# A GNN kernel on one core: one edge tile in 75 of the two relation passes fetched by 128 row DMAs on ScalarE's queue

## The chip, the core and the metric

One core of one Trainium2 chip runs one program. Its engines are TensorE (PE; PEld is its weight load), VectorE (DVE), ScalarE (ACT), GpSimd (POOL) and SyncE (SP), and 16 DMA engines move data between the chip's memory and the core. Each engine works through its own queue of instructions in program order and waits on semaphores. The metric is the device time of one execution in microseconds (us); lower is better.

## What is computed

A graph with N = 30,000 nodes of 128 features and E = 960,000 edges, sorted by destination. Two layers, both with a layer norm, a relu and a residual:

```python
h = relu(layernorm(x))
# layer 0, run twice (basis1, then basis2 on relu of the first result): the two relation passes
W   = einsum('rb,bdf->rdf', coeff, basis)          # 32 relations from 8 bases
msg = einsum('nd,rdf->nrf', h, W)[src, etype] * norm
agg = segment_sum(msg, dst, N) + bias
# layer 1: the gate pass, 4 edge types
msg = sigmoid(k[dst] + q[src]) * v[src];  out = mean over types of (segment_sum(msg, dst) + x @ Ws + b)
```

The part that matters here: for every edge of a relation pass, the feature row of its source node has to be fetched from a table in memory.

## The kernel before

After a short preparation (up to 190 us) three passes over all edges follow: c1 (relation pass 1, reads table h0), c2 (relation pass 2, reads h1) and g (the gate). Only c1 and c2 are changed.

**Tiles.** 128 edges make a tile (TP), 3 tiles a group (G), 5 groups a block (S), 5 blocks a stage (SB; 25 groups, 75 tiles = NTS), 4 stages a loop iteration (NQ), and each pass is a loop of 25 iterations (NI). So a pass has 7,500 tiles, 2,500 groups, 500 blocks and 100 stages. The 384 sorted edges of a group fall into a window of 32 neighbouring destination nodes. The order of work within an iteration is written out by hand: the body below is unrolled, and each engine gets its instructions in that order.

**A group, in `rel_body`.** GpSimd issues three gathers (L118): each takes a column of 128 source indices and fetches 128 rows of 512 bytes into one third of the tile hg, which has 5 buffers, that is 15 gathers. VectorE builds for each tile a matrix sb (L476, 12 buffers): edge by (basis, window column), filled with the edge's coefficient. TensorE multiplies hg by sb and adds the group's three tiles in the PSUM tile pa (L481, 3 buffers). ScalarE copies pa into the block's tile ab (L485). A gather can start when the matmuls of the group five earlier have released its hg buffer; a matmul needs its gather, its sb and a free pa.

**A block.** After the second group of block s+1, TensorE runs the 8 basis matmuls of block s (bases_out, L440), which read the whole ab of block s. VectorE later adds the result into the aggregate (L374). In c1 each block also needs its relation types: four SP DMAs load er for block s+2 at the start of block s (types, L397), VectorE turns er into a one-hot at the fourth group of block s (L405), TensorE multiplies it by the coefficients (L410), and ScalarE stores half of the result for pass 2 (keep, L430). In c2 that result is read back by one SP DMA a block (L435).

**Beside it.** Every 9 or 10 groups a node step of 120 finished nodes is spread over the next groups (`after_first`, `after_second`): transposes, activations on ScalarE (L608, L617; in c2 L653, L661, L672, L685) and stores on ScalarE's queue (L621; in c2 two of L692). SP loads the index tiles of a stage one stage ahead (L351, L357). Eight semaphores are handed in turn to the DMAs of SP and ScalarE: a DMA waits until the eighth before it, in the order in which the program was written, has landed.

The loop over the groups of a block, cut:

```python
for j in range(G):
    gather(hg[:, j, :], table, idx[:, t0 + j:t0 + j + 1])
...
nc.scalar.copy(ab[s][:, :, g, :], pa)
if g == 1 and s:
    bases_out(s - 1)
...
beside(s * S + g)
```

Of the kernel before, what the change touches and what calls it, by code (L numbers as in the profile page):

```python
# [9 lines left out]
F32 = mybir.dt.float32  # L10
I32 = mybir.dt.int32
# [10 lines left out]
N = 30000  # L22
# [8 lines left out]
TP = 128  # L31
NT = E // TP
G = 3
# [3 lines left out]
S = 5  # L37
SB = 5
NQ = 4
NS = NQ * SB  # L40
NGS = S * SB
NTS = NGS * G
# [8 lines left out]
LEAD = 3 * VB  # L51
GAP = 8
EPS = 1e-5
CH = 5
PX, KX = 120, 10
IN_RANGE = "destinations are node numbers, below N"


def rows_of(col, n):
# [13 lines left out]
def kernel(  # L73
# [29 lines left out]
    nc = tc.nc  # L103
# [192 lines left out]
    def sorted_path():  # L296
# [5 lines left out]
        with ExitStack() as all_:  # L302
# [57 lines left out]
            def bases(t, engine):  # L360
# [2 lines left out]
                    min_val=0, max_val=N - 1, skip_runtime_bounds_check_because=IN_RANGE)  # L363
                return vals

            def edge_row(row, i, s, n):

                return bass.AP(tensor=row.tensor, offset=(i * NG + s * S) * GE,
                               ap=[[0, n], [GE, S], [1, GE]])
# [6 lines left out]
            def rel_body(table, weights, second):  # L376
# [4 lines left out]

                def body(bas, i, io, pool, ps, cp, iw, ic, beside):
                    stage = {}
                    er, oh, pc, ce, ce_next, ab, po, base = {}, {}, {}, {}, {}, {}, {}, {}

                    def loads(k):
                        stage[k] = [stage_tile(io, "idx", src, I32, i, k),
                                    stage_tile(io, "relc", reld, F32, i, k),
                                    firsts(io, i, k)]
                        if not second:  # L390
                            stage[k].append(
                                stage_tile(io, "nrm", norm, F32, i, k, 4 * TQ - S * G))

                    def types(s):
                        er[s] = pool.tile([P, TQ, TP], I32, name="er")
                        for c in range(TQ):
                            nc.sync.dma_start(  # L397
                                er[s][:, c, :],
                                bass.AP(tensor=et32_row.tensor,
                                        offset=(i * NG + s * S) * GE + c * TP,  # L400
                                        ap=[[TQ * TP, 4], [0, R], [1, TP]]))

                    def onehot(s):
                        oh[s] = pool.tile([P, TQ, TP], F32, name="oh")
                        nc.vector.tensor_scalar(oh[s], er[s], icol4, None, op0=ALU.is_equal)  # L405
                        at = TQ * 8 * B
                        pc[s] = cp[:TP, at:2 * at].rearrange("p (c q l b) -> p c q l b", c=TQ, q=4,
                                                             l=2)
                        for c in range(TQ):
                            nc.tensor.matmul(pc[s][:, c].rearrange("p q l b -> p (q l b)"),  # L410
                                             lhsT=oh[s][:, c, :],
                                             rhs=coeff.rearrange("p q l b -> p (q l b)"),
                                             start=True, stop=True)

                    def coefficients(s):
                        t0 = s % SB * S * G
                        nrm = stage[s // SB][-1][:, t0:t0 + 4 * TQ]
                        for to, l in ((ce, 0), (ce_next, 1)):
                            to[s] = pool.tile([TP, 4, TQ, B], F32, name=f"ce{l}")
                            nc.vector.tensor_mul(  # L420
                                to[s], pc[s][:, :, :, l].rearrange("p c q b -> p q c b"),
                                nrm.rearrange("p (q c) -> p q c", q=4).unsqueeze(3).to_broadcast(
                                    [TP, 4, TQ, B]))
                            to[s] = to[s].rearrange("p q c b -> p (q c) b")

                    def block_rows(s):
                        return ce2[ds(i * NS + s, 1)].rearrange("o p e -> (o p) e")

                    def keep(s):
                        nc.scalar.dma_start(block_rows(s), ce_next[s][:, :S * G, :].rearrange(  # L430
                            "p t b -> p (t b)"))

                    def kept(s):
                        ce[s] = pool.tile([TP, S * G, B], F32, name="ce", bufs=4)
                        nc.sync.dma_start(ce[s].rearrange("p t b -> p (t b)"), block_rows(s))  # L435

                    def bases_out(s):
                        po[s] = ps.tile([P, S, W], F32, name="po")
                        for b in range(B):
                            nc.tensor.matmul(po[s].rearrange("p s w -> p (s w)"),  # L440
                                             lhsT=bas[:, b, :],
                                             rhs=ab[s][:, b].rearrange("p s w -> p (s w)"),
                                             start=(b == 0), stop=(b == B - 1))

                    loads(0)
                    if second:
                        kept(0)
                        kept(1)
                    else:
                        types(0)  # L450
                        onehot(0)
                        coefficients(0)
                        types(1)
                        onehot(1)
                    for s in range(NS):
                        k = s // SB
                        if s % SB == 0:
                            if s:
                                tc.stage_boundary()
                            if k + 1 < NQ:  # L460
                                loads(k + 1)
                        if s % SB == 2:
                            leave_stage()
                        idx, relc, start = stage[k][:3]
                        if s + 2 < NS:
                            (kept if second else types)(s + 2)
                        ab[s] = pool.tile([P, B, S, W], F32, name="ab")
                        for g in range(S):
                            t0 = (s % SB * S + g) * G
                            hg = pool.tile([TP, G, D], F32, name="hg", bufs=5)  # L470
                            for j in range(G):
                                gather(hg[:, j, :], table, idx[:, t0 + j:t0 + j + 1])
                            pa = ps.tile([P, B, W], F32, name="pa", bufs=3)
                            for j in range(G):
                                sb = pool.tile([TP, B, W], F32, name="sb", bufs=12)
                                nc.vector.scalar_tensor_tensor(  # L476
                                    sb, iw[:TP].unsqueeze(1).to_broadcast([TP, B, W]),
                                    relc[:, t0 + j:t0 + j + 1],
                                    ce[s][:, g * G + j, :].unsqueeze(2).to_broadcast([TP, B, W]),
                                    op0=ALU.is_equal, op1=ALU.mult)  # L480
                                nc.tensor.matmul(pa.rearrange("p b w -> p (b w)"),  # L481
                                                 lhsT=hg[:, j, :],
                                                 rhs=sb.rearrange("p b w -> p (b w)"),
                                                 start=(j == 0), stop=(j == G - 1))
                            nc.scalar.copy(ab[s][:, :, g, :], pa)  # L485
                            if g == 1 and s:
                                bases_out(s - 1)
                            if g == 2 and not second and s + 1 < NS:
                                coefficients(s + 1)
                            if g == 3 and not second:  # L490
                                keep(s)
                                if s + 2 < NS:
                                    onehot(s + 2)
                            if g == 3 and s > 1:
                                add_windows(po[s - 2], base[(s - 2) // SB], s - 2)
                            if g == 3 and s % SB == 1:
                                base[k] = bases(start, DVE)
                            beside(s * S + g)
                    bases_out(NS - 1)
                    for s in (NS - 2, NS - 1):  # L500
                        add_windows(po[s], base[NQ - 1], s)
# [500 lines left out]
```

## Time and profile before

| What | us |
|---|---|
| median of 10 runs (lowest to highest) | 33,972.54 (33,958.92 to 34,021.55) |
| the profiled execution, its own time | 33,968.25 |
| its span, first to last instruction | 33,966.5 |
| c1: first to last gather start | 190.2 to 11,532.2 |
| c2: first to last gather start | 11,566.9 to 22,437.6 |
| gate pass: first to last gather start | 22,483.3 to 33,934.9 |

The profile is of one execution. In its lists of instructions a row gives the line, the engine, the operation, out<-in by tile name and the count; then busy time, the mean of one, and the idle time just before them with what ended it. "issue" means that nothing the profile shows was waited for, "remote" that a semaphore event without a matching instruction ended the wait. POOLq, SPq and ACTq are instructions of the queues themselves, such as issuing a DMA. The ends of matmuls are modelled, so TensorE's times are rough.

### The profile page before, as it was taken

What the parts mean: (1) busy time and instruction counts of PE and PEld (TensorE: products, weight loads), DVE (VectorE), ACT (ScalarE), POOL (GpSimd) and SP (SyncE); (2) the same over time, 40 slices, a digit from 0 to 9 for tenths busy, and PEclk for the clock granted to TensorE, in tenths of its full rate; (3) what the DMA queues carried; (4) which work ended last, traced back from release to release, by engine and by line L of the source; (5) the groups of instructions that cost most, each with busy time, mean ns of one, the idle gap of its engine ahead of it and who ended that gap; (6) DMA issues with size and microseconds to landing.
All of it is one profiled execution on the core that took longest, in us unless ns stands there. A gap on an engine that the chain in (4) does not pass through costs nothing.

```text
span 33966.5 us, 321519 instructions
## 1 busy us (share of the span) xinstructions
PE 19883.3 (59%) x83304; PEld 16939.1 (50%) x83304; DVE 12380.0 (36%) x32695; ACT 3633.4 (11%) x9834; POOL 21302.7 (63%) x22514
## 2 busy tenths in 40 slices
PE   4555555555555566666666666655555555555555
PEld 3444444444444444444444444445555555555555
DVE  3333333333333333333333333333333333333333
ACT  1000000000000011111111111111111111111111
POOL 5666666666666666666666666666666666666665
PEclk8777777777777777877777777765555555555555
DMA  3222222222222222222222222234444444444444
GB/s 98 63 63 64 64 64 64 63 62 65 64 64 64 66 66 66 66 67 66 66 66 66 66 67 66 67 98 125 124 124 124 124 124 125 124 124 124 124 124 120
DMA packets 2171202, 2914.97 MB, mean 86 GB/s; under 512 B 684764, under 2 KB 1617880, under 8 KB 2169544
## 3 DMA queue, kind: packets, MB, share of 16 engines
q0 software_dynamic: 840000, 1967.52, 21.8%
q1 hardware_dynamic: 923347, 651.19, 6.6%
q10 hardware_dynamic: 406197, 276.11, 2.8%
q8 instruction: 802, 13.14, 0.2%
q14 instruction: 856, 7.01, 0.1%
HBM read 2618.79 MB, written 274.16 MB: 85 GB/s over the span
## 4 chain that ended last, share of the span: by engine, by line


## 5 line engine op out<-in xcount | busy, mean ns | idle before, releaser
L118 POOL DMA_INDIRECT hg<-h,idx x15000 | 14186.9, 946 | 8223.8 <-issue 4295.6
L481 PE MATMUL pa<-sb,hg 128*128 128x256 f32 x30000 | 9196.2, 464 | 6068.2 <-issue 3822.4
L481 PEld LDWEIGHTS pa<-sb,hg 128*128 128x128 f32 x30000 | 6891.9, 239 | 7875.0 <-issue 4269.9
L118 POOL DMA_INDIRECT qv<-qvtab,qi x7500 | 7088.8, 945 | 4408.5 <-issue 2284.9
L476 DVE SCALAR_TENSOR_TENSOR sb<-cp,relc,ce 128x256 f32<-128x256 f32 x15000 | 6139.6, 477 | 5429.8 <-remote 4443.3
L549 PE MATMUL po<-sel,msg 128*128 128x32 f32 x15000 | 3456.2, 387 | 4606.2 <-DVE msg L547 3852.9
L549 PEld LDWEIGHTS po<-sel,msg 128*128 128x128 f32 x15000 | 3419.6, 327 | 4896.6 <-DVE msg L547 4020.3
L538 PE MATMUL pk<-kw,oh 128*128 128x128 f32 x15000 | 3969.1, 438 | 142.3 <-issue 97.7
L579 DVE TENSOR_TENSOR pk<-pk,qv 128x384 f32<-128x384 f32 x2500 | 1408.3, 563 | 7093.4 <-remote 5123.6
L485 ACT COPY ab<-pa 128x256 f32<-128x256 f32 x5000 | 1810.4, 373 | 19841.0 <-remote 9586.4
L538 PEld LDWEIGHTS pk<-kw,oh 128*128 128x128 f32 x15000 | 3463.1, 331 | 145.0 <-issue 145.0
L440 PE MATMUL po<-ab,bas 128*128 128x160 f32 x16000 | 2517.5, 313 | 418.4 <-issue 275.9
L440 PEld LDWEIGHTS po<-ab,bas 128*128 128x128 f32 x16000 | 2429.5, 201 | 543.7 <-issue 324.9
L374 DVE TENSOR_TENSOR agg<-agg,po 128x32 f32 x7500 | 1404.0, 187 | 2608.9 <-ACT xs L653 672.0
L580 ACT ACTIVATE pk<-pk 128x384 f32<-128x384 f32 x2500 | 1187.4, 475 | 9392.8 <-DVE pk L579 6157.5
L676 PE MATMUL bank<-wall,hT 128*120 128x512 f32 x1524 | 1042.7, 807 | 944.8 <-DVE kt L687 275.8
L547 DVE TENSOR_TENSOR msg<-pk,qv 128x384 f32<-128x384 f32 x2500 | 1370.2, 549 | 0.0
L410 PE MATMUL cp<-coeff,oh 128*128 128x64 f32 x4000 | 653.7, 304 | 782.7 <-issue 610.3
L525 DVE TENSOR_TENSOR oh<-kb,cp 128x1920 f32<-128x1920 bf16 x500 | 1073.2, 2146 | 47.6 <-issue 31.9
L410 PEld LDWEIGHTS cp<-coeff,oh 128*128 128x128 f32 x4000 | 653.6, 228 | 860.2 <-issue 763.4
L687 DVE TENSOR_TENSOR kt<-bank,ball 120x512 f32<-120x512 f32 x254 | 175.7, 692 | 2267.4 <-PE bank L676 946.7
L676 PEld LDWEIGHTS bank<-wall,hT 128*120 128x120 f32 x1524 | 350.1, 247 | 1278.5 <-issue 629.7
(77 smaller groups left out, 3381.5 us busy)
## 6 DMA issues: line engine op xcount, KB each, us to landing
hg<-h,idx POOLq DMA_INDIRECT x15000
kb<-kcode SPq DMA_DIRECT2D x500, 480.0 KB
kw<-ktab SPq DMA_DIRECT2D x2500, 64.0 KB
er<-in_et_row SPq DMA_DIRECT2D x2000, 64.0 KB
qvtab<-qvt ACTq DMA_DIRECT2D x254, 480.0 KB
qv<-qvtab,qi POOLq DMA_INDIRECT x7500
ktab<-kt ACTq DMA_DIRECT2D x254, 240.0 KB
ce<-ce ACTq DMA_DIRECT2D x500, 60.0 KB
```

The lines of the kernel that those rows point to most:

```text
L118: nc.gpsimd.indirect_dma_start(out=to, out_offset=None, in_=table, in_offset=bass.IndirectOffsetOnAxis(ap=idx, axis=0))
L374: nc.vector.tensor_add(to, to, po[:, g, :])
L410: nc.tensor.matmul(pc[s][:, c].rearrange("p q l b -> p (q l b)"), lhsT=oh[s][:, c, :], rhs=coeff.rearrange("p q l b -> p (q l b)"), start= ...
L440: nc.tensor.matmul(po[s].rearrange("p s w -> p (s w)"), lhsT=bas[:, b, :], rhs=ab[s][:, b].rearrange("p s w -> p (s w)"), start=(b == 0), ...
L476: nc.vector.scalar_tensor_tensor(sb, iw[:TP].unsqueeze(1).to_broadcast([TP, B, W]), relc[:, t0 + j:t0 + j + 1], ce[s][:, g * G + j, :].uns ...
L481: nc.tensor.matmul(pa.rearrange("p b w -> p (b w)"), lhsT=hg[:, j, :], rhs=sb.rearrange("p b w -> p (b w)"), start=(j == 0), stop=(j == G ...
L485: nc.scalar.copy(ab[s][:, :, g, :], pa)
L538: nc.tensor.matmul(pk[n][:, j, :], lhsT=oh[n // S][:, n % S, j * TP:(j + 1) * TP], rhs=kw[n], start=True, stop=True)
L547: nc.vector.tensor_mul(msg, pk[n], qv[n][:, :, 1, :])
L549: nc.tensor.matmul(po[s][:, g, :], lhsT=msg[:, j, :], rhs=sel[s][:, g * G + j, :], start=(j == 0), stop=(j == G - 1))
L579: nc.vector.tensor_add(pk[n], pk[n], qv[n][:, :, 0, :])
L676: nc.tensor.matmul(bank(a, VB, T * D), lhsT=hT, rhs=wall[:, a].rearrange("p t f -> p (t f)"), start=True, stop=True)
```

## The change

In each stage of both relation passes the last of the 75 tiles is no longer gathered by GpSimd. At the stage's first group SP loads that tile's 128 indices into a row (ix). After the copy of each of the first 21 groups (NGX), ScalarE issues 6 or 7 DMAs, one row of 512 bytes each, from the table into a tile hx; before every 16th row it loads 16 indices into registers. The matmul of the last tile reads hx in the place of hg. The other passes and all arithmetic stay.

```diff
+XR = 16
+NGX = NGS - 4
...
+            def last_tile(io, pool, table, array, i, k):
+                ix = io.tile([1, TP], I32, name="ix")
+                nc.sync.dma_start(
+                    ix, array[:, ds(i * (NQ * NTS) + (k + 1) * NTS - 1, 1)].rearrange("p o -> o p"))
+                to = pool.tile([TP, table.shape[1]], F32, name="hx")
+                vals = []
+
+                def fetch(n):
+                    for p in range(n * TP // NGX, min((n + 1) * TP // NGX, TP)):
+                        if p % XR == 0:
+                            _, vals[:] = nc.values_load_multi_w_load_instructions(
+                                ix[:, p:p + XR], engines=[mybir.EngineType.Activation], min_val=0,
+                                max_val=table.shape[0] - 1,
+                                skip_runtime_bounds_check_because=IN_RANGE)
+                        nc.scalar.dma_start(to[p:p + 1, :], table[ds(vals[p % XR], 1), :])
+
+                return to, fetch
...
                             hg = pool.tile([TP, G, D], F32, name="hg", bufs=5)
+                            rows = [hg[:, j, :] for j in range(G)]
+                            if t0 == 0:
+                                last[k] = last_tile(io, pool, table, src, i, k)
+                            if t0 + G == NTS:
+                                rows[-1] = last[k][0]
                             for j in range(G):
-                                gather(hg[:, j, :], table, idx[:, t0 + j:t0 + j + 1])
+                                if t0 + j + 1 < NTS:
+                                    gather(rows[j], table, idx[:, t0 + j:t0 + j + 1])
...
-                                                 lhsT=hg[:, j, :],
+                                                 lhsT=rows[j],
...
                             nc.scalar.copy(ab[s][:, :, g, :], pa)
+                            last[k][1](s % SB * S + g)
                             if g == 1 and s:
                                 bases_out(s - 1)
```

More of the change, by code (lines that the diff above doesn't have):

```diff
@@ L53 @@
 EPS = 1e-5
+XR = 16
+NGX = NGS - 4
 CH = 5
 PX, KX = 120, 10
-IN_RANGE = "destinations are node numbers, below N"
+IN_RANGE = "the edges' ends are node numbers, below N"
 def rows_of(col, n):
@@ L383, in body @@
                     stage = {}
-                    er, oh, pc, ce, ce_next, ab, po, base = {}, {}, {}, {}, {}, {}, {}, {}
+                    er, oh, pc, ce, ce_next, ab, po, base, last = {}, {}, {}, {}, {}, {}, {}, {}, {}
                     def loads(k):
```

## Prediction

> **What bounds the kernel now.** I began with the page's groups by cost and its line of engine totals, to see which engine sets the pace of a pass.
>
> ```profile
> PE 19883.3 (59%) x83304; PEld 16939.1 (50%) x83304; DVE 12380.0 (36%) x32695; ACT 3633.4 (11%) x9834; POOL 21302.7 (63%) x22514
> ...
> L118 POOL DMA_INDIRECT hg<-h,idx x15000 | 14186.9, 946 | 8223.8 <-issue 4295.6 <-remote 2207.4 <-PE pa L481 1206.4
> ```
>
> No engine is full. But GpSimd's gathers of the two relation passes are 14,186.9 us of work with 8,223.8 us of idle time before them: together they fill the 22,212.7 us from the first gather to the last of each pass (190.2 to 11,532.2 and 11,566.9 to 22,437.6). Of the idle time 4,295.6 us is "issue": the fixed pause of some 0.30 us after each gather. Next the timeline of GpSimd's queue around 5,000 us, which shows the rhythm.
>
> ```profile
> 5004.94 0.94 POOL L118 DMA_INDIRECT hg<-h,idx  x1 [0.31 <-issue]
> 5006.19 0.95 POOL L118 DMA_INDIRECT hg<-h,idx  x1 [0.30 <-issue]
> 5010.95 0.94 POOL L118 DMA_INDIRECT hg<-h,idx  x1 [3.82 <-remote]
> 5012.20 0.94 POOL L118 DMA_INDIRECT hg<-h,idx  x1 [0.30 <-issue]
> ```
>
> A gather every 1.25 us, then a stall of 3.8 us, then gathers again. From 5,010.95 to the next stall it is 15 gathers, one block, exactly the five buffers of hg. Over a pass the pitch is 11,342.0/7,499 = 1.512 us in c1 and 10,870.7/7,499 = 1.450 us in c2, so a block takes 22.7 and 21.7 us, of which 15 x 1.25 = 18.75 are gathers and 3.9 and 3.0 stalls. GpSimd waits there for TensorE to release hg. So the bound is a loop: gathers at their own pace as far as the buffers reach, then a wait for the slower side (TensorE, VectorE, ScalarE), once a block.
>
> **The change, removed.** Per stage one gather; 200 in both passes. At the unhindered pitch 200 x 1.25 = 250 us. Ends: 100 x 1.512 + 100 x 1.450 = 296 us if stalls shrink with the gathers, and 0 if the other side of the loop sets the block, since then only the stall grows. I take 250: the trace's gathers stand back to back within a run.
>
> **Added on ScalarE.** No single-row DMA stands on ScalarE's queue before. These are the nearest rows: one-row DMAs on SP (firsts, L357), full tiles on ScalarE (L430), and the one register load on ScalarE (L251).
>
> ```profile
> L357 SPq DMA_DIRECT2D firsts<-in_first_st x300: 3/284/714, 188.0 to 33722.6; - x150
> ...
> L430 ACTq FUSED_REGOPS  x500: 52/55/60, 224.4 to 11535.2; - x167
> ...
> L430 ACTq MOVE ce<-ce x500: 29/29/35, 224.7 to 11535.4; - x167
> L430 ACTq DMA_DIRECT2D ce<-ce x500: 337/338/389, 224.8 to 11535.5; - x167
> ...
> L251 DVEq TENSOR_LOAD <-flag x1: 1908/1908/1908, 174.8 to 174.8; - x1
> L251 ACTq TENSOR_LOAD <-flag x1: 1281/1281/1281, 179.3 to 179.3; - x1
> ```
>
> The columns are least/median/greatest ns. A row needs an address (start to start of the next instruction 84 ns), a move (70 ns), the DMA and about 40 ns to the next: 0.194 + 0.284 = 0.478 us with SP's median; 0.25 us for the DMA (its shorter undisturbed cases) gives 0.444, ScalarE's 0.338 gives 0.532. I take 0.478, since size, not engine, separates the two rows. 128 rows are 61.2 us. Eight register loads of 16 values: 8 x 1.281 = 10.2 us (ends: 8 x 0.478, SP's load of the same flag, = 3.8; 8 x 1.846, VectorE's median for 25 values, = 14.8). So 71.4 us a stage, in 21 of its 25 groups. Those last 21 x 4.54 = 95 us in c1 and 21 x 4.35 = 91 us in c2. The engine's own work there is small (1,014 us busy in 11,300 of c1, 1,160 in 10,800 of c2), and register work and DMA issues run while a copy runs. ScalarE becomes some 75 to 85% occupied in those groups. It does not become the bound by sum, only by order: each copy now stands behind 6 or 7 rows of the group before.
>
> A page speaks here. The Trainium skill, "DMA: Bandwidth & Descriptors", section "Latency and other measured facts", puts the floor of a register load at about 0.6 us; ScalarE's one row here shows 1.281, and the measurement decides. With the page's figure the loads would be 4.8 us a stage in place of 10.2. Its section "Issuing engines are not separate DMA queues" says that starting DMAs from several engines saves only the sequencer's time of starting them, which it calls usually small; here the row of L118 shows 0.946 us of that time for a gather.
>
> **What waits behind the rows.** TensorE needs the copies in two places: pa has three buffers, and the basis matmuls L440 read ab of the whole block. I replayed the trace's start times of ScalarE's instructions with 6 or 7 rows (and the register loads) put behind every copy. A copy starts 2.2 us (c1) and 2.5 us (c2) later on average, at worst some 9 us in 99 of 100. That is later than the trace's matmul three groups on in 8% and 13% of groups, by 0.08 and 0.24 us a group averaged over all; and L440 would start 0.59 us later a block in c1 and 0.67 in c2. As full prices, since L440 stands in front of the matmuls that release the hg buffer that the gathers wait for: 500 x 0.59 + 500 x 0.67 = 630 us. Ends: 0 (the wait that releases hg ends later than L440 anyway) and, with the slow ends of row and load (0.532 and 1.85), 500 x 1.23 + 500 x 1.72 = 1,475 us. I take 630, nearest to the rows chosen.
>
> **SP's queue.** The index row is one more DMA a stage: it is issued after er's at the first group and has from 1 us (the first stage of an iteration) to 28 us and more before the copy that it is needed behind; bounds 0 and 25 x 2 x 5 us = 250, taken as 0. More serious: the eight shared DMA semaphores tie SP to ScalarE. Before, the last er DMA of block s+2 was issued 37.5 us (median, least 19.8) ahead of its one-hot. After, it must wait until the first rows of the group before block s have landed.
>
> ```profile
> 5014.37 0.37 ACT L485 COPY ab<-pa 128x256 f32<-128x256 f32 x1 [2.83 <-PE pa L481]
> ...
> 5017.12 0.48 DVE L405 TENSOR_SCALAR oh<-er,icol 128x512 f32<-128x512 int32 x1
> ```
>
> The copy is that of the last group of block s-1; the one-hot of block s+2 starts 2.8 us after it (median of the trace; 4.6 in the upper quarter). Four er DMAs cannot be issued and landed in 2.8 us: SP's own DMA row L397 has a median of 549 ns and its moves go up to 1.6 us. So this one-hot will wait perhaps 5 to 10 us a block in c1. It costs nothing as long as VectorE's next sb of that block waits for TensorE anyway, as in the block shown, where it starts 16 us later. Bounds 0 and 450 x 10 = 4,500 us; in the forecast 0, in the third case below more.
>
> **Sum.** -250 + 630 = +380 us on the execution's 33,968 us: 34,350 us. That execution is 4 us under the median of the runs, so the sum holds for the median too.
>
> **Rivals.** (1) The rows hide altogether: TensorE's release of hg does not depend on the copies at the margin. For it: within a run GpSimd never waits for ScalarE (36 us of waits on L485 in c1), the stalls cluster at 2 to 3.5 us whatever precedes them, and ScalarE's register and DMA instructions show no slow cases (52/55/60). Then -250 us, 33,720 us. (2) Gain and delay cancel: half of L440's delay counts, -250 + 315 = +65, 34,030 us. (3) The one-hot's wait comes on the path: VectorE stands at L405, and sb, L410 and the adds behind it. It decides from the point where er lands later than VectorE would have gone on, about 16 us after L405. At 3 us for each of 450 blocks: +1,350 on top, some 35,700 us. Against it: the slack shown. (4) The change does not do what it says: the instruction order shows 74 gathers a stage in place of 75 and 512 row DMAs an iteration on ScalarE, so I give this nothing.
>
> **Chances.** Forecast 0.44; (1) 0.33; (2) 0.10; (3) 0.13. About 0.2% (68 us) is what a measurement can tell from no change. Faster is case (1), 0.33; same is case (2), 0.10; slower is the forecast and (3), 0.57. The forecast's own range is 34,050 to 35,200 (380 less 300 from half the delay hidden, and 1,475 - 250 at the slow ends). The range over the cases reaches down to case (1), 33,690, and up to 35,200, leaving out case (3) and a few hundredths on either side.
>
> **What would show it.** Right: GpSimd's gathers 14,800 with the same 0.945 us, stalls a block longer than 3.9 and 3.0 us; TensorE's L440 and L481 idle before them with ScalarE as releaser, more than the 1,200 us of now; a row DMA of 0.28 to 0.34 us and a register load near 1.3 us on ScalarE. Wrong, for case (1): the pitch of the gathers within a run unchanged and the stalls no longer, the passes 125 us shorter each. For case (3): waits of VectorE's L405 on the DMA er, now 19 us in all, in the thousands, in c1 alone. A row DMA that costs 0.1 us, or one that ScalarE has to wait for, would make the working wrong in either direction.

## The result and the profile after

On the chip of the profile the changed kernel takes **37,326.04 us** (median of 8 runs, 37,286.87 to 37,348.27) beside 33,986.94 for the kernel before: 1.0981 of it, 95% interval 1.0971 to 1.0990. The profiled execution took 37,297.57 us, its span 37,295.8. The forecast was 34,350 and the range ended at 35,200. The direction was right, the size was not.

One thing must be known to read the rest. The sets of experiments ran on different chips, all runs of a set on one. On some chips the kernel before takes 33,970 to 34,380 us (the profile's is one of them), on others 28,430 to 28,500. I call them the first and the second kind. A ratio is always to the kernel before on the same chip.

The page of the changed kernel first: the gathers, and the matmuls that use them (busy time, mean ns, idle time before them and what ended it).

```profile
L120 POOL DMA_INDIRECT hg<-h,idx x14800 | 14032.0, 948 | 11710.0 <-PE pa L509 4673.5
L509 PE MATMUL pa<-sb,hg 128*128 128x256 f32 x29600 | 9126.6, 465 | 4938.3 <-issue 3202.5
```

200 gathers are gone and the others cost what they did, but the idle time before them grew from 8,224 to 11,710 us, and what ends most of it is now the matmul L509 (4,674 us; the same matmul, L481, ended 1,206 before). c1 took 12,768 us in place of 11,342 from first to last gather, c2 12,763 in place of 10,871; a stage 127.7 us in both. The list of waits says why TensorE is late (total us, times, longest).

```profile
ACT ab L513 <- DMA hx<-h: 5941.1, 1195, 15.4
...
POOL hg L120 <- PE pa L509: 4673.5, 1213, 12.1
...
DVE ce L442 <- DMA ce<-ce: 2300.9, 190, 19.9
...
PE bank L685 <- ACT xs L682: 1906.3, 160, 21.6
...
PEld pa L509 <- ACT ab L513: 1525.1, 394, 14.2
...
PEld po L462 <- ACT ab L513: 1392.4, 248, 16.6
...
PE bank L705 <- ACT hT L701: 1304.1, 128, 14.8
```

Read it from the bottom: TensorE waits for ScalarE's copy L513, for a free pa and for ab, and in c2 for two activations of the node step, xs and hT; the copy waits behind the row DMAs of its own queue (5,941 us); and VectorE's L442 waits for the DMA of keep, which ScalarE now issues behind rows too. The first wait for an activation was much shorter in the kernel before:

```profile
PE bank L656 <- ACT xs L653: 726.9, 98, 13.7
```

TensorE's added waits lie in different places in the two passes. In c1 the matmuls' waits for copies (L509 and L462) grew from 811 to 2,068 us. In c2 they hardly grew, from 429 to 537, but the waits for xs and hT together went from 983 to 3,207; and c2 is the pass that lost more, 1,893 us beside 1,426. Now the rows themselves (least/median/greatest ns).

```profile
L384 ACTq FUSED_REGOPS  x25600: 1/37/1730, 219.6 to 25778.0; - x199
L384 ACTq MOVE hx<-h x25600: 1/29/1644, 219.7 to 25778.1; - x199
L384 ACTq DMA_DIRECT2D hx<-h x25600: 1/227/1452, 220.4 to 25778.1; - x199
```

The medians are as cheap as one could wish. The greatest values are not: register instructions of 1.7 us. The timeline of ScalarE shows what that makes of a group's rows.

```profile
5010.99 2.29 ACTq L384 DMA_DIRECT2D hx<-h  x7
...
5014.39 5.78 ACTq L384 DMA_DIRECT2D hx<-h  x5
5020.50 0.37 ACT L513 COPY ab<-pa 128x256 f32<-128x256 f32 x1 [5.88 <-issue]
5020.90 10.61 ACTq L384 DMA_DIRECT2D hx<-h  x7
...
5032.16 0.37 ACT L513 COPY ab<-pa 128x256 f32<-128x256 f32 x1 [11.29 <-DMA hx<-h]
5032.31 2.23 ACTq L384 DMA_DIRECT2D hx<-h  x6
```

Seven rows in 2.29 us, then seven in 10.61, with the next copy 11 us late. And GpSimd in the same stretch:

```profile
5011.67 0.95 POOL L120 DMA_INDIRECT hg<-h,idx  x1 [2.98 <-remote]
...
5027.37 0.95 POOL L120 DMA_INDIRECT hg<-h,idx  x1 [0.31 <-issue]
5028.62 0.95 POOL L120 DMA_INDIRECT hg<-h,idx  x1 [0.30 <-issue]
5038.51 0.95 POOL L120 DMA_INDIRECT hg<-h,idx  x1 [8.95 <-PE pa L509]
```

The first seven rows began in GpSimd's pause and ended 1.6 us after it, the slow ones came while it gathered back to back, and the quick ones from 5,032 us on came in its next pause. Over the whole trace, the pitch from one row to the next in a run of rows is 0.42 us on the mean within 2 us after GpSimd resumes, and 1.2 to 1.8 us some 10 to 12 us after it, by how long a pause has to be to count. Rows and register loads filled ScalarE for 98.3 us a stage.

### The profile page after: what moved, and what is told of

The parts are those of the page before. It is cut to its first block, busy times and chain, and to the rows that moved or that the text cites. A ratio compares the mean times of both kernels' runs of the same rounds, so it can differ in the third digit from the quotient of the medians.

```text
span 37295.8 us, 399832 instructions
## 1 busy us (share of the span) xinstructions
PE 20434.7 (55%) x83304; PEld 17230.9 (46%) x83304; DVE 12376.2 (33%) x32695; ACT 3699.5 (10%) x9834; POOL 21169.1 (57%) x22314
## 4 chain that ended last, share of the span: by engine, by line
## 5 line engine op out<-in xcount | busy, mean ns | idle before, releaser
L120 POOL DMA_INDIRECT hg<-h,idx x14800 | 14032.0, 948 | 11710.0 <-PE pa L509 4673.5
L509 PE MATMUL pa<-sb,hg 128*128 128x256 f32 x29600 | 9126.6, 465 | 4938.3 <-issue 3202.5
L509 PEld LDWEIGHTS pa<-sb,hg 128*128 128x128 f32 x29600 | 6784.6, 239 | 6799.3 <-issue 3928.0
L462 PE MATMUL po<-ab,bas 128*128 128x160 f32 x16000 | 2904.6, 345 | 1716.6 <-ACT ab L513 1252.5
L462 PEld LDWEIGHTS po<-ab,bas 128*128 128x128 f32 x16000 | 2770.0, 226 | 1966.0 <-ACT ab L513 1392.4
L513 ACT COPY ab<-pa 128x256 f32<-128x256 f32 x5000 | 1847.3, 371 | 17712.2 <-DMA hx<-h 5941.1
L705 PE MATMUL bank<-wall,hT 128*120 128x512 f32 x1524 | 1136.8, 874 | 1956.5 <-ACT hT L701 1304.1
L685 PE MATMUL bank<-ident,xs 128*120 128x128 f32 x254 | 108.7, 430 | 2234.8 <-ACT xs L682 1906.3
L442 DVE TENSOR_TENSOR ce<-cp,nrm 128x128 f32<-128x128 f32 x1000 | 265.9, 285 | 3096.5 <-DMA ce<-ce 2300.9
```

The source lines that it names most:

```text
L120: nc.gpsimd.indirect_dma_start(out=to, out_offset=None, in_=table, in_offset=bass.IndirectOffsetOnAxis(ap=idx, axis=0))
L462: nc.tensor.matmul(po[s].rearrange("p s w -> p (s w)"), lhsT=bas[:, b, :], rhs=ab[s][:, b].rearrange("p s w -> p (s w)"), start=(b == 0), ...
L509: nc.tensor.matmul(pa.rearrange("p b w -> p (b w)"), lhsT=rows[j], rhs=sb.rearrange("p b w -> p (b w)"), start=(j == 0), stop=(j == G - 1))
L705: nc.tensor.matmul(bank(a, VB, T * D), lhsT=hT, rhs=wall[:, a].rearrange("p t f -> p (t f)"), start=True, stop=True)
```

## The experiments

The theories. **A**: while GpSimd gathers, the instructions of ScalarE's queue can take 0.7 us and more each, so rows cost far more than their median. **B**: the rows cost what the forecast says, and the copies behind them are late. **C**: the DMAs, their landing or the semaphores that they share cost the time. Later A1 (register instructions) against A2 (register loads), and **A3** (nothing is lost until ScalarE is full) against **A5** (what counts is how many rows lie between two copies).

### First set (chip of the first kind, before 34,288.62)

**One DMA in place of 128** (one_dma). The row numbers ix and their loads go too.

```diff
-                        nc.scalar.dma_start(to[p:p + 1, :], table[ds(vals[p % XR], 1), :])
+                nc.scalar.dma_start(to, table[0:TP, :])
```

> Leaves out: the right rows of the 75th tile. The 200 gathers stay away, but the tile is filled by one DMA of 128 neighbouring rows of the table per stage on ScalarE's queue; no row numbers, no register loads, no single rows. It prices the removal alone. Both theories below take the removal for a gain: 200 gathers x 1.25 us = 250 us off 33,987, so 33,740 (33,690 to 33,860). Rival R0, that the last group's matmul on the separate tile or GpSimd's missing gather itself makes the loop slower: above 33,990, up to the 37,326 of the change.

Measured 34,172.42 us, 0.9963 (0.9949 to 0.9978). The removal is worth a gain, about half of that expected: -116 us of -250. The stalls of c1 (idle beyond the 1.25 us pitch) are 2,182 us, beside 1,982 and 2,060 in the two profiles of the kernel before; those are of other chips, so that the stalls took the rest back is likely, not shown.

**Rows from fixed places** (rows_const), without row numbers and loads.

```diff
- nc.scalar.dma_start(to[p:p + 1, :], table[ds(vals[p % XR], 1), :])
+ nc.scalar.dma_start(to[p:p + 1, :], table[7 * p:7 * p + 1, :])
```

> Leaves out: the row numbers; the 128 rows come from fixed places of the table. 128 single-row DMAs a stage as in the change, in the same places behind the copies, but without register loads and without the two register instructions ahead of each DMA. Theory A (while GpSimd gathers, every instruction of ScalarE's queue can take 0.7 us; the mean pitch of rows in the changed kernel is 0.709 us against 0.39 in the fast cases, three instructions a row): one instruction a row, 0.26 us fast, plus a third of the excess of 0.32 us, is about 0.36 us, 47 us a stage in place of 101, so most of the loss goes: 34,000 to 34,800. Theory C (the DMAs themselves, their landing or the semaphores they share, cost the time, not their instructions): as many DMAs, so 36,500 or more. Theory B (only the order at the row price of the prediction): 33 us a stage in place of 71, 33,740 to 34,100.

Measured 34,378.11 us, 1.0029 (1.0020 to 1.0039), 46 us of rows a stage. The row's line, from the instructions of its source line (least/median/greatest ns):

```profile
L376 ACTq DMA_DIRECT2D hx<-h x25600: 3/261/1678, 216.3 to 22698.2; - x199
```

As many DMAs landed in as many rows of hx, and nine tenths and more of the loss are gone: between one_dma and the change lie 1.0981 - 0.9963 = 0.102 of before (the change's figure is of the profile's chip), between one_dma and this 0.0066. So C falls: neither the DMAs nor their landing make the loss. It comes with the register loads and the two register instructions ahead of each DMA.

**The copies on VectorE** (copy_dve).

```diff
- nc.scalar.copy(ab[s][:, :, g, :], pa)
+ nc.vector.tensor_copy(ab[s][:, :, g, :], pa)
```

> The change as it is, with the ab copy of each group moved from ScalarE to VectorE, so that no copy stands behind rows. Theories A and B (the loss comes over the copies that wait behind rows): TensorE's waits for the copy of some 1,200 to 1,500 us and GpSimd's waits for the pa matmul of 4,673 us fall back to the 1,206 of before; ScalarE's 101 us of rows and loads fit beside a stage of 113 us; what stays is VectorE's added 25 copies of about 0.37 us a stage and the after-work of ScalarE behind rows: 33,900 to 35,000. Theory C (DMAs, landing, shared semaphores): the wait stays where it is, 36,500 or more.

Measured 36,524.87 us, 1.0654 (1.0636 to 1.0672). The microseconds reach theory C's 36,500 by a hair, but this chip is slower; on the scale of the first chip's 33,987, on which the expectations were worked out, it is 36,210, between the two, and both miss. From its list of waits:

```profile
DVE ab L513 <- PE pa L509: 8017.6, 3613, 16.9
ACT r L637 <- DMA hx<-h: 5819.0, 158, 93.6
```

VectorE now stands 8,018 us before its copies, a wait that the edit made itself, so it isn't a clean test. The second line is the useful one: with no copy left on it, ScalarE is still behind (its after-work waits up to 94 us behind rows). Its queue is taken for 119 of 126 us a stage in c1; but that counts waits among the rows, whose DMAs start 25 us a stage after the instruction ahead of them has ended, up to 21 us at once, beside 13 us a stage in the change. What they waited for was not followed. So the copies' place is not the whole loss, against B.

**No gathers** (no_gathers).

```diff
- gather(rows[j], table, idx[:, t0 + j:t0 + j + 1])
+ nc.gpsimd.memset(rows[j], 0.5)
```

> Leaves out: all 14,800 gathers of the two relation passes; GpSimd fills each tile with a constant by a memset instead. Rows, loads and copies as in the change. It shows ScalarE's rows without GpSimd's gathers. Theory A (the gathers slow the queue's instructions): the row pitch has no slow cases, 0.38 to 0.42 us on the mean against 0.709, the DMA instruction about 0.23 us, and the largest below 0.6. Rival A2 (ScalarE's queue slows by itself when it issues densely): mean pitch stays at 0.6 us or more, with cases of 0.7 and 1.4 us. The passes get shorter in either case, to 80 to 100 us a stage by A, bound by ScalarE or VectorE.

The instructions of the rows' line:

```profile
L384 ACTq FUSED_REGOPS  x25600: 37/37/47, 208.9 to 17586.4; - x199
L384 ACTq MOVE hx<-h x25600: 29/29/43, 209.0 to 17586.5; - x199
L384 ACTq DMA_DIRECT2D hx<-h x25600: 217/234/1302, 209.1 to 17586.6; - x199
```

On the chip on which the other runs of the set show slow cases (a fifth of SP's register instructions over 0.3 us in one_dma), the rows' register instructions have a greatest of 47 ns without the gathers, where the changed kernel had 1,730. SP's tell the same within this one run: none of 7,516 took over 0.3 us in the two relation passes, and 985 of 6,592 in the gate pass, which kept its gathers. The mean pitch in a run of rows is 0.450 us (expected 0.38 to 0.42; A2's 0.6 or more is out). Theory A stands: the gathers make the rows slow, not the density of the queue. Single DMA instructions still went up to 1.3 us, which the expectation of 0.6 did not have. The run, a single execution, took 29,246 us, some 87 us a stage.

### Second and third sets (chips of the second kind, before 28,432.9 and 28,434.3)

They were meant to tell A1 from A2, and came on chips where the loss does not exist.

**One register load a stage** (one_load), used for every 16 rows:

```diff
-                        if p % XR == 0:
+                        if p == 0:
```

> Leaves out: 112 of the 128 row numbers; the 16 first are loaded once a stage and used again for every 16 rows. So 1 register load a stage in place of 8, and as many rows, each with its two register instructions. All numbers on the scale of 33,987 for before. Theory A1 (the 256 register instructions a stage, slowed while GpSimd gathers, are what fills ScalarE): 9 us of 98 a stage go, the time stays at 36,300 to 37,200. Theory A2 (the register loads, each of which stops the queue until it is back, and the row numbers they wait for): 34,100 to 34,700. Theory A3 (what counts is how full ScalarE is in a stage, from whatever it comes, with a steep rise near full): between, 35,300 to 36,600.

**Loads without their use** (loads_only):

```diff
-                        nc.scalar.dma_start(to[p:p + 1, :], table[ds(vals[p % XR], 1), :])
+                        nc.scalar.dma_start(to[p:p + 1, :], table[7 * p:7 * p + 1, :])
```

> Leaves out: the use of the row numbers; rows come from fixed places as in the run with constant rows, but the row numbers are fetched and the 8 register loads a stage are made as in the change. Theory A1 (register instructions): 34,100 to 34,600, about 0.3 per cent above before as without loads, plus at most 1 per cent. Theory A2 (register loads): 36,500 or more. Theory A3 (how full ScalarE is): 56 us a stage, 34,100 to 34,700.

**Half the rows** (half_rows):

```diff
+                nc.scalar.dma_start(to[TP // 2:], table[TP // 2:TP, :])
...
-                    for p in range(n * TP // NGX, min((n + 1) * TP // NGX, TP)):
+                    for p in range(n * TP // 2 // NGX, min((n + 1) * TP // 2 // NGX, TP // 2)):
```

> Leaves out: rows 64 to 127 of each 75th tile, which one DMA of 64 neighbouring rows fills. 64 single rows a stage with their register instructions and 4 loads, spread over the same groups. About 49 us of ScalarE a stage in place of 98. If every row costs alike (the loss of 17 us a stage is shared by the rows): 35,400 to 35,900. If the loss comes only from a ScalarE that is nearly full (A3), 33,900 to 34,600, like the run with constant rows, whose ScalarE had 46 us a stage.

**The rows on SP** (rows_sp):

```diff
-                                ix[:, p:p + XR], engines=[mybir.EngineType.Activation], min_val=0,
+                                ix[:, p:p + XR], engines=[mybir.EngineType.SP], min_val=0,
...
-                        nc.scalar.dma_start(to[p:p + 1, :], table[ds(vals[p % XR], 1), :])
+                        nc.sync.dma_start(to[p:p + 1, :], table[ds(vals[p % XR], 1), :])
```

> The change with its rows and register loads on SP's queue in place of ScalarE's, in the same places of the program order; it computes what the change computes. If the loss comes over ScalarE's copies and after-work that stand behind rows, it is gone with them, and SP, with about 100 us of rows and 30 loads in a stage of 113, still hands over in time: 33,800 to 34,900. If the rows' issue fills whatever queue they are put on, SP's one-hot rows, indices and kept coefficients land late and the loss stays or grows: 36,500 to 40,000.

Measured: one_load 0.9910 (0.9893 to 0.9926), loads_only 0.9912 (0.9896 to 0.9929), half_rows 0.9937 (0.9921 to 0.9954), rows_sp 1.0728 (1.0710 to 1.0746). The first two are the removal and nothing else, and half_rows falls short of it by 0.003, so they tell nothing between A1, A2 and A3. The surprise is the gathers: they run at 1.249 us with hardly a stall in all three. rows_sp is the one that loses. From its list of waits:

```profile
DVE oh L427 <- DMA er<-in_et_row: 3441.7, 362, 18.6
...
PE pa L509 <- DMA hx<-h: 2234.4, 125, 24.5
```

The one-hots wait for relation types that SP fetches behind rows, and the last matmul of a stage for rows that come late: the mechanism of the prediction's third rival, but with the rows on the other queue. SP itself is not slowed here (no register instruction over 0.2 us); it had waits of its own in front of the rows, 2,495 us of them for the store of ktab, which ScalarE issues.

**The change itself, once more**, with one_load beside it.

> The changed kernel itself, beside before on the chip of this call, since before took 28,433 us on the chip of the second set of experiments and 33,987 and 34,289 on those ahead of it, and the gathers of that set ran at 1.249 us without stalls. On a chip where before takes about 34,000: 1.09 to 1.10 of before, as first measured. On one where it takes about 28,400: theory A (the slowed queue instructions, which come with GpSimd's stalls and did not show in that set: row pitch 0.447 us) gives the removal alone, 250 us of 28,433, so 28,180, 0.991 of before. A rival, that the eight register loads or the registers cost their time on any chip, gives 1.03 to 1.10 there too.

> The kernel with one register load a stage in place of eight, beside the changed kernel. Leaves out 112 of the 128 row numbers. On a chip where before takes about 34,000: theory A1 (register instructions) 1.065 to 1.095 of before; theory A2 (register loads) 1.00 to 1.02; theory A3 (how full ScalarE is) between. On one where it takes about 28,400: 0.991 again, which tells nothing between them.

Measured **28,188.12 us, 0.9913 (0.9897 to 0.9930)**, and one_load 0.9910 again. The same program that loses 9.8% on the first chip gains 0.9% here: 28,434.3 - 28,188.1 = 246 us, the 200 gathers of 1.25 us. Its page, and the instructions of the rows' line:

```profile
L120 POOL DMA_INDIRECT hg<-h,idx x14800 | 13997.9, 946 | 4718.4 <-issue 3636.3
```

```profile
L384 ACTq FUSED_REGOPS  x25600: 37/37/47, 209.2 to 18737.7; - x199
L384 ACTq MOVE hx<-h x25600: 29/29/41, 209.3 to 18737.7; - x199
L384 ACTq DMA_DIRECT2D hx<-h x25600: 217/227/1216, 209.4 to 18737.8; - x199
```

A gather takes the same 946 ns; the idle time before it is 4,718 us, little more than the 0.30 us pause of each. And the rows have the same medians as on the first chip, without the slow cases. Nor do the transfers differ: the packets of ScalarE's DMA queue took 2.9% of 37,296 us in the change on the first chip and 3.8% of 28,185 here, about 1,080 and 1,070 us. The granted TensorE clock does differ, 0.673 there and 0.739 here, but it goes with the time and not with the kind of chip: rows_twice below has 0.668 on a chip of the second kind. Summed over the trace to the start of the next instruction, a stage's rows and loads take (us):

| | first chip, changed kernel | this chip, same kernel |
|---|---|---|
| address (FUSED_REGOPS) | 21.5 | 8.8 |
| MOVE | 23.7 | 12.6 |
| DMA | 42.8 | 35.1 |
| 8 register loads | 10.2 | 11.2 |
| sum, with semaphores | 98.3 | 67.8 |

Of the 30.5 us that the first chip adds, 24 are register instructions, 8 the DMA instructions, and the loads none. That speaks for A1 against A2. No run with fewer loads was made on a chip of the first kind (one_load stands at 0.9910, 0.9910, 0.9912 and, in a single execution, 28,182 us, all on the second), so it is read from the trace and not shown by an edit.

### Fourth to sixth sets (second kind, before 28,496, 28,434 and 28,439)

If the loss is a full ScalarE, it can be made on a chip of the second kind with more rows.

rows_twice fetches every row again, rows_200 those with p % 16 under 9, into a tile hy that nobody reads:

```diff
                         nc.scalar.dma_start(to[p:p + 1, :], table[ds(vals[p % XR], 1), :])
+                        if p % XR < 9:
+                            nc.scalar.dma_start(too[p:p + 1, :], table[ds(vals[p % XR], 1), :])
```

> The change with every row fetched a second time, into a tile that nobody reads: 256 rows a stage, and as many register instructions again. Theory A3 (rows cost nothing until ScalarE is full, then everything): where before takes about 28,400, ScalarE needs 256 x 0.393 + 10 = 111 us for rows and loads and 9 us for copies in a stage that GpSimd does in 92.5, so a stage grows to 115 to 130 us, 200 x 22 to 37 us more than the changed kernel: 32,600 to 35,700, 1.15 to 1.26 of before, though the same 128 rows once cost nothing there (0.991). Where before takes about 34,000 the rows take 0.7 us, 190 us a stage: 1.4 to 1.7 of before. If rows cost little by number (no full engine), 1.00 to 1.05 where before takes 28,400.

> The change with 72 of the 128 rows of a stage fetched a second time, into a tile that nobody reads: 200 rows a stage. Where before takes about 28,400 a row took 0.42 to 0.44 us, so rows and loads take about 97 us of ScalarE a stage, as much as the 128 slow rows took in the changed kernel's first profile (98.3). Theory A3 (the loss of the change is nothing but those 98 us of ScalarE a stage): the loss per stage is that of the first measurement, 17 us over the removal alone, so 28,180 + 200 x 10 to 20 = 30,200 to 32,200, 1.06 to 1.13 of before. Rival A4 (98 us would still fit; the late hand-overs between engines of that chip were needed too): 0.99 to 1.03. Where before takes about 34,000: 1.25 to 1.45.

rows_twice: 36,663.59 us, **1.2867** (1.2845 to 1.2888). rows_200: 32,567.17 us, **1.1455** (1.1436 to 1.1474). Both go beyond A3's range, by 0.03 and 0.015, and far beyond the rivals'. 128 rows cost nothing, 200 cost 4,379 us more than those, 256 another 4,096. rows_200 gives ScalarE 96 us of rows and loads a stage, without one slow register instruction (the line of the added rows):

```profile
L387 ACTq FUSED_REGOPS  x14400: 37/37/43, 209.3 to 23111.2; - x198
L387 ACTq MOVE hy<-h x14400: 29/29/38, 209.4 to 23111.6; - x198
```

and its list of waits resembles that of the changed kernel, on another chip:

```profile
ACT ab L516 <- DMA hx<-h: 7228.1, 1524, 13.0
...
POOL hg L120 <- PE pa L512: 3480.1, 1752, 8.2
DVE ce L445 <- DMA ce<-ce: 3440.5, 300, 16.9
...
PEld pa L512 <- ACT ab L516: 3149.4, 1169, 7.1
```

The last three keep the number of rows and change only how many groups they lie in.

The edit of rows_13; rows_24, and rows_200_24 with 200 rows, have NGS - 1 (24 groups):

```diff
-NGX = NGS - 4
+NGX = NGS - 12
```

> The change with its 128 rows spread over the first 13 groups of a stage in place of 21, 10 behind a copy in place of 6. Theory A5: the copies stand behind the rows, so a stage takes, in the groups with rows, ScalarE's rows, loads and copies, and in the others GpSimd's 3.7 us a group. Where before takes about 28,400: 68 + 13 x 0.37 + 12 x 3.7 = 117 us in place of 92.5, 24 us a stage, less some 5 us that buffers lend (200 rows: 119 by this sum, 114 measured): 28,180 + 200 x 20 to 25 = 32,200 to 33,200, 1.13 to 1.17. Theory A3 in its plain form (only ScalarE's total in a stage counts; 68 + 9 of 92.5 us): 0.99 to 1.00, as with 21 groups. Where before takes about 34,000: A5 98 + 5 + 12 x 4.5 = 157 us a stage in place of 113, 1.25; plain A3 1.10.

> The 200 rows a stage of the run ahead of this, spread over 24 groups in place of 21. Where before takes about 28,400: theory A5, 96 + 24 x 0.37 + 1 x 3.7 = 109 us a stage in place of 119 by the same sum, so 10 us less than the measured 114: 104 to 109 us, 28,180 + 200 x 12 to 16 = 30,600 to 31,400, 1.075 to 1.105. Plain A3: no change, 1.145. Against both: the rows of the last groups land too late for the last matmul, which adds a wait of about 2 us a stage, 400 us, to either. Where before takes about 34,000: no more than 0.05 below the run with 200 rows on 21 groups, 1.2 to 1.4.

> The change with its 128 rows spread over 24 groups in place of 21, 5 or 6 behind a copy. It computes what the change computes. Where before takes about 34,000: theory A5, 98 + 24 x 0.37 + 4.5 = 112 us a stage, about the 113 and 109 of before, so most of the loss goes: 1.00 to 1.04. Plain A3: 1.10 as in the change. Where before takes about 28,400: 0.991, or up to 1.005 if the last rows land late.

Measured 1.0696 (1.0631 to 1.0760) for 13 groups; 1.1653 (1.1583 to 1.1724) for 200 rows on 24; 0.9935 (0.9913 to 0.9957) for the change on 24. Neither theory has all three. rows_13 says that the place counts even where ScalarE is not full: plain A3 had 0.99 to 1.00, A5 1.13 to 1.17. A5's sum was 117 us a stage, the trace has 104, so the buffers lend 13 us and not the 5 that I allowed. The stalls stand in groups 12 to 19, at the end of the rows, not among the first. rows_200_24 is against A5: spread wider, the rows cost more, not less. What TensorE waited for at the matmul L512 in it (matmuls and weight loads together; us, times) has a new entry:

```profile
  ACT ab L516: 5263.1, 1986
  issue: 3635.1, 1740
  DMA hx<-h: 1151.4, 177
```

1,151 us for rows of hx that the last group's matmul needs and that are issued only a group earlier. ScalarE was full on 21 groups already, and a full engine isn't helped by spreading. All runs but rows_13 follow ScalarE's sum. In us a stage, from the traces, c1/c2 (waiting is any gap over 0.3 us that doesn't stand among rows):

| kernel, kind of chip | rows and loads | its other work | stage | to before |
|---|---|---|---|---|
| before, first | 0 | 12/16 | 113.4/108.7 | 1 |
| rows_const, first | 52/40 | 9/15 | 113.9/110.9 | 1.0029 |
| **the change, first** | 101/94 | 11/15 | 127.7/127.6 | 1.0981 |
| **the change, second** | 72/64 | 8/14 | 92.8/92.4 | 0.9913 |
| rows_13, second | 70/65 | 10/15 | 103.9/104.1 | 1.0696 |
| rows_200, second | 101/91 | 8/13 | 114.8/113.9 | 1.1455 |
| rows_200_24, second | 101/92 | 8/14 | 117.0/117.8 | 1.1653 |
| rows_twice, second | 122/114 | 7/12 | 137.2/132.1 | 1.2867 |

With 200 and 256 rows ScalarE waits only 6 to 12 us a stage: it is the bound, and the stage is little more than its sum. The change on the first chip has 112 and 109 us of ScalarE's work, as much as a whole stage of before (113.4 and 108.7), which leaves no room for any wait. On the second kind it has 80 of 92.5 us, which still fits, with little room; rows_13, with as much, shows that fitting is not enough when the rows stand close.

**Before, profiled again**, on a third chip of the first kind, took 34,375.03 us.

> The kernel before, profiled on the chip of this call. If before takes about 28,400 here: theory A (the loss is a property of the chip first measured, on which GpSimd's gathers stall because other engines' queue instructions and hand-overs come late) wants, in the same program, gathers at 1.25 us with idle before them of about 0.3 us each, 4,500 us for 15,000 in place of 8,224, passes of 9,370 us in place of 11,342 and 10,871, the same 946 ns a gather, and SP's register instructions followed without the 0.7 us steps. Rival: the gathers themselves are shorter there, below 900 ns. If before takes about 34,000 here, it repeats the first profile.

Its group of gathers:

```profile
L118 POOL DMA_INDIRECT hg<-h,idx x15000 | 14220.0, 948 | 8411.6 <-issue 4141.5 <-remote 2473.0 <-PE pa L481 1079.6
```

It repeats the first profile: 948 ns a gather, 8,412 us of idle. So there is no profile of the kernel before on the second kind: only its time there, and the gathers almost without stalls of its near relatives one_load, loads_only, half_rows and the change.

## Why the prediction was wrong

**The step that failed is "Added on ScalarE"**, the row at 0.478 us with ends 0.444 and 0.532, and its conclusion: "It does not become the bound by sum, only by order." On the chip of the profile a row took (98.3 - 10.2)/128 = 0.688 us on the mean, outside both ends; ScalarE then had some 110 us of work a stage, as much as a whole stage of before, so it did reach the bound by sum. On chips of the second kind the same step is good, so its size is the first chip's: 0.442 us a row, 67.8 us a stage beside the forecast 71.4. What misled it was the sentence in rival (1) that ScalarE's instructions show no slow cases (52/55/60). That row was true and measured little: 500 instructions, one a block. SP's row in the same fence, 3/284/714, showed the mark of slow cases, and I used its median. From start to start L357's three instructions took 448, 365 and 469 ns on the mean in the kernel before, where their medians are 108, 68 and 337: so the warning was in the trace, 1.28 us in place of 0.51, though well above the 0.688 that came. A median prices a row that is alone; a hundred rows in sequence cost the mean under the load that they will meet.

**Removed, -250.** Half right: -116 us on a chip of the first kind (0.9963), -246 with the rows on one of the second. In the first, part of the gathers' time probably came back as stalls, towards the end 0 that the text named.

**What waits behind the rows, +630 with ends 0 and 1,475.** The chain was the right one in c1, TensorE waiting for copies that stand behind rows: over both passes its wait for L513 at the basis matmuls rose from 141 to 1,253 us, and GpSimd's for L509 from 1,206 to 4,674. In c2 it was not: the prediction looked for the copies alone, and put at nothing the node step's activations, which stand on the same queue and which TensorE awaited for 3,207 us in place of 983. How much of that reached the end of the pass no edit has shown. The size followed from the wrong row. Against one_dma, rows and loads cost 0.102 x 33,987 = 3,460 us.

**The loads, 10.2 us a stage.** Right: 10.2 measured, 1.27 us each. The page named there, the Trainium skill's "DMA: Bandwidth & Descriptors", has about 0.6 us for one (section "Latency and other measured facts"); on ScalarE no undisturbed load of these runs is below 1.05 us, while SP's load of one value in the kernel before took 0.478. Its section "Issuing engines are not separate DMA queues" calls the saved time of starting DMAs usually small; here 128 starts, with their addresses and loads, are 68 to 98 us a stage and decide the sign.

**SP's queue, 0, and rival (3).** The one-hots L427 waited 19 us for er in all, as before, so rival (3) did not come. What did come is next to it and was not priced: L442's wait for the store of keep, 2,301 us, since that store's DMA is issued on ScalarE's queue behind rows.

**Rivals (1) and (2).** Rival (1), all hidden, -250: wrong on the profile's chip, and exactly what happens on chips of the second kind. Rival (2), +65, came on neither. That the chip could change the sign was in none of the cases.

**What would show it.** The marks held as far as they went: 14,800 gathers of 948 ns, longer stalls, TensorE's waits for ScalarE above 1,200 us, a load near 1.3 us. The row DMA of 0.28 to 0.34 us did not: 0.227 us at the median, with a tail to 1.45 us. The last sentence named that, "one that ScalarE has to wait for", as what would make the working wrong, but gave it no price.

**What stays open.** Why chips of the two kinds differ isn't known; the runs show only where (the same 946 to 948 ns a gather, but slow register instructions beside it and long stalls before it). Whether fewer register loads would help on the first kind was not run there. In the changed kernel on the first chip ScalarE still waited 16 to 19 us a stage, more than in rows_200 (6 to 10), so late hand-overs from TensorE probably add to the loss; that is argued, not shown. rows_24 on a chip of the first kind, where it might help, wasn't tried there.

## What to carry to other kernels

Price work that is put on a queue by the mean and the tail of that instruction under the load that it will run beside, never by the median of a rare one; an address instruction that takes 66 ns at the median, up to the start of the next, took 168 on the mean here. Then add up the engine that gets it, stage by stage, with all that it does already: it cost nothing here while it fitted with room, and its whole excess and more from then on (128 rows nothing; with 200 rows, in c1, 109 us of ScalarE where a stage had been 92.8 made a stage of 114.8). Many instructions between two copies on an in-order queue cost something even before that: 13 groups in place of 21 cost 8%. Look at everything that waits on that queue, not only at the instruction beside the new work: in c2 TensorE's added waits were for the node step's activations and hardly for the copies. And of two versions within a few per cent, the better one can depend on the chip; measure on more than one.

## What the runs showed of the hardware

- Two kinds of chip, by the kernel before: 33,970 to 34,380 us on three sets, 28,430 to 28,500 on five. In all traces a gather takes 944 to 949 ns. On the first kind 17 to 21% of SP's register instructions in before, one_dma and the change take over 0.3 us, on the second at most 3 of 14,108 in a run, the longest 0.37 us.
- On the first kind the slow cases come with the gathers: ScalarE's register instructions had 8.3% over 0.3 us in the change, none with memsets in place of gathers, and SP's had none in the relation passes then, but 15% in the gate pass, which kept its gathers.
- A slow case mostly takes some 0.7 us whatever the instruction does: of ScalarE's register instructions over 0.3 us in the change, 86% take 0.65 to 0.75, in the slow stretches of the timeline above many DMA and register instructions stand at 0.69 to 0.71 us, and 7 rows of three instructions take 10.61 us where 7 took 2.29.
- A row DMA with a fixed address took 0.26 us of ScalarE's queue at the median (first kind); with an address from a register 0.39 us from row to row, three instructions.
